# Cross-attention block with an MLP in f32: fc_w's forty-nine-product operands made during attention, and one fc scheme for all four MLP groups

## The chip, the cores and the metric

The kernel runs on one core of a Trainium2 chip. The metric is device time in microseconds; lower is better. All arithmetic is in f32. PE is the matrix engine (TensorE), PEld its weight loads, DVE the vector engine, ACT the scalar engine, POOL the GpSimd engine; SP issues the DMAs, and SPq is its queue.

## The reference

A transformer layer with cross-attention over 8 sequences of 256 tokens, width 512, 16 heads of 32, and an MLP of inner width 2048. Here x and ctx are [8, 256, 512]:

```python
y = layer_norm(x, ln1_w, ln1_b)
q = y @ q_w + q_b                      # [8,256,512] -> 16 heads of 32
k, v = ctx @ k_w + k_b, ctx @ v_w + v_b
attn = softmax(q @ k^T / sqrt(32) + mask)
hidden = (attn @ v) @ cproj_w + cproj_b + x
y = layer_norm(hidden, ln2_w, ln2_b)
y = gelu(y @ fc_w + fc_b, approximate=True)     # fc_w [512, 2048]
return hidden + y @ proj_w + proj_b             # proj_w [2048, 512]
```

## The kernel before

The 2048 tokens are worked in four groups of 512 (two sequences each). The kernel has two phases: attention for all four groups, and then the MLP for all four groups.

**Matrix products.** A product of two matrices cut into quarters is made with seven quarter products in place of eight (Winograd's form of Strassen's scheme). The left operand's quarters are 11, 12, 21, 22; `A_SUMS` makes from them four sums, called s3, s2, (a new) 21 and s4, and `B_SUMS` makes t1, t2, (a new) 12 and t4 of the right operand. `sum_up(eng, x, table, i)` issues sum i on the engine given. An operand of seven parts for 512 × 512 weights is a tile [128, 7, 2, 256], 1792 KB in all.

fc is a product of fc_w with the group's y. In group 0 of the MLP it is made column quarter by column quarter of fc_w (`fcw[0]` to `fcw[3]`): for each of four quarters q, seven products of 16 matmuls with 256 token columns. In groups 1 to 3 the scheme is applied twice: seven outer products of seven inner ones, 49 in all, each of 4 matmuls with 128 token columns. The profile shows two rows for every f32 matmul: 224 rows for the 7 × 4 × 4 of group 0, 392 for the 49 × 4 of another group. For these, fc_w's operands are the outer seven sums, each with its own inner seven parts: `w2`, seven operands of 1792 KB. They are made during group 0's MLP by `split_sums` on DVE and POOL through a stage tile `w_stage`, stored to `w2_dram` (L979, L980) and by `keep_quarters` (L989, L990), and loaded by `load_w2(g, k)` (L1004 to L1008) after each outer product for the product four further on.

**Buffers.** The weight pool has one tag with four buffers of 1792 KB. In attention they hold kw, qw, vw and cw (cproj_w); then come the four `fcw`, then `w2`.

**Attention.** It is a loop over 32 units n = (group g, head group hg, sequence b), eight units u = 2·hg + b for each group. A unit makes the scores of unit n+2 on PE (L575), softmaxes on DVE and ACT (L593, L603), a division on POOL (`divide`, L617), transposes of the probabilities on PE (`turn_probs`, L628), and the product with v (`attend`, L644; ACT writes it into the attention buffer, L652). The order is written out by hand: `aside[g, u, i]` holds work to be issued in slot i of a unit, and `between[g, u, i]` holds pieces of the projections for PE. `begin(g, u, i, f)` appends to a slot:

```python
for n, (g, hg, b) in enumerate(units):
    scores(n + 2); softmax(n + 2, 0)
    run(aside[g, u, 0])
    turn_probs(n, 0); turn_probs(n, 1); divide(n + 1)
    softmax(n + 2, 1); softmax(n + 2, 2)
    run(between[g, u, 0])
    turn_probs(n, 2); turn_probs(n, 3)
    run(aside[g, u, 1]); softmax(n + 2, 3)
    run(between[g, u, 1]); run(aside[g, u, 2])
    attend(n)
    run(later); run(aside[g, u, 3])
```

Each engine works through its instructions in this order. SP issues all DMAs, also in this order, and there are at most eight in flight: the issue of a DMA waits for the one eight before it. Keys, queries and values are stored to DRAM by `store_quarter` (L423) and loaded by `load_qk` (L511) and `load_v` (L516) for the head group that needs them. The attention output of group 1 is spilled (`spill_att`, L699) and reloaded chunk by chunk into `att_in` (`reload_att`, L704); its sums are made on POOL (L171), and `sum_att` (L664) makes those of a group whose output stays. The output projection (cw) of groups 1 and 2 runs as pieces in the fourth group's units. The residual x is loaded in quarters (`load_res`, L546), gets its bias on POOL (`bias_res`, L552) and is stored as `hid_dram` (L560). In the fourth group, hid of group 0 is loaded again (`hm`, L179), normalised on DVE and turned, to be y of MLP group 0.

**MLP.** For each group: fc (lines L926 on PE, L929 for the additions on DVE and POOL), gelu on ACT, then the product with proj_w, whose sums `pw_sums` are made during group 0. proj_w is loaded at the phase's start (L935). `add` and `mm` are helpers, so that many operations stand under one line and are told apart by their tiles.

Of the kernel before, what the change touches and what calls it, by code (L numbers as in the profile page):

```python
# [16 lines left out]
P = 128  # L17
# [5 lines left out]
def tile_xattn_block(  # L23
# [78 lines left out]
    }  # L102
    att_dram = tc.dram_tile([P, NHG, G], F32, name="att_dram")
# [37 lines left out]
    def weight(name, w, f=0):  # L141

        a = Operand(wts.tile([P, 7, HC, S], F32, tag="w", bufs=4, name=name))
        load_quarters(a, w, f, QUARTERS)
        return a

    def load_quarters(a, w, f, which):
        step = HI if w.shape[1] > D else S
        src = w.rearrange("(c p) n -> p c n", p=P)
        for n, k, at in (("11", 0, 0), ("12", HC, 0), ("21", 0, 1), ("22", HC, 1)):  # L150
            at = f + at * step
            if n in which:
                nc.sync.dma_start(a[n], src[:, k : k + HC, at : at + S])

# [81 lines left out]
    ys, hids, fcw = {}, {}, {}  # L236
# [15 lines left out]
    with ExitStack() as att:  # L252
# [98 lines left out]
        turns, later, waiting = [0], [], []  # L351
# [404 lines left out]
        for g in range(NG):  # L756
# [8 lines left out]
        spread(0, [(6, 2), (6, 2), (7, 2), (7, 2)], [lambda i=i: sum_up(GP, ws["c"], A_SUMS, i) for i in ALL])  # L765
# [14 lines left out]
            [(u, i, 1) for u in range(8) for i in range(2) if (u, i) not in ((6, 1), (7, 1))],  # L780
# [15 lines left out]
        for c, (u, i) in enumerate(((6, 1), (6, 1), (7, 1), (7, 1))):  # L796
            between[g, u, i].append(lambda c=c: th(c))

        def load_fc(q):
            fcw[q] = weight(f"fcw_{q}", fc_w, q * S)  # L800

        for q in (0, 2, 1):
            begin(g, 0, 3, load_fc, q)
        spread(
            g,
            [(2, 2), (2, 3), (4, 2), (5, 2)],
            [lambda i=i: sum_up(GP, fcw[0], A_SUMS, i) for i in ALL],
        )
# [7 lines left out]
        for t in range(12):  # L816
            nc.tensor.transpose(warm[:, ts(t % NT, P)], ident, ident)

        ws["k"] = Operand(wts.tile([P, 7, HC, S], F32, tag="w", bufs=4, name="kw"))
        ctxs[0] = load_tiles(  # L820
            work, group_of(ef, 0), "ctx", "ctx_0", lambda: load_quarters(ws["k"], k_w, 0, ("11", "12"))
        )
        load_quarters(ws["k"], k_w, 0, ("21", "22"))
        load_x(0)
        ws["q"] = weight("qw", q_w)
        load_mask(0)
        ws["v"] = weight("vw", v_w)
        for to, vec in ((cb, cproj_b), (projb, proj_b)):
            nc.sync.dma_start(to, vec.partition_broadcast(P))

# [5 lines left out]
        ws["c"] = weight("cw", cproj_w)  # L836
# [61 lines left out]
        sum_att(3, NHG - 1, V)  # L898
        for i in ALL:
            run(o[i : i + 1])  # L900
            sum_up(V, ys[0], B_SUMS, i)
# [3 lines left out]
        load_fc(3)  # L905


    with ExitStack() as mlp:
# [25 lines left out]
        for n, f, d in (("11", 0, 0), ("12", 0, HD2), ("22", HF, HD2), ("21", HF, 0)):  # L934
            nc.sync.dma_start(  # L935
                pw[n], proj_w.rearrange("(c p) n -> p c n", p=P)[:, f : f + HF, d : d + HD2]
            )

        def sum_pw():
# [12 lines left out]
        pw_sums = sum_pw()  # L952
        pbd = wpool.tile([P, HD2], F32, name="pbd")
        add(GP, pbd, projb[:, :HD2], projb[:, HD2:], ALU.subtract)

        w2_dram = tc.dram_tile([7, P, 7, HI // 2], F32, name="w2_dram")
        stage = wpool.tile([P, 3, 4, S], F32, tag="y2", bufs=1, name="w2_stage")
        FC_ORDER = (  # L960
            ("11", "11"), ("12", "21"), ("s2", "t2"), ("s3", "12"), ("21", "t1"), ("s4", "22"), ("22", "t4")
        )
        stages, staged_sums = [0], {}

        def split_sums(eng, n, r, half=None):
            a, b = fcw[r][n], fcw[r + NQF // 2][n]
            if half != 1:
                staged_sums[n, r] = stage[:, stages[0] % 3]
                stages[0] += 1
            st = staged_sums[n, r]  # L970
            s1, s2, s3, s4 = (st[:, i, :] for i in range(4))
            if half != 1:
                add(eng, s3, a[:, 0, :], b[:, 0, :], ALU.subtract)
                add(eng, s2, b[:, 1, :], s3, ALU.subtract)
            if half != 0:
                add(eng, s1, s2, a[:, 0, :])
                add(eng, s4, a[:, 1, :], s2, ALU.subtract)
                to = w2_dram[QI[n]][:, :, r * S : (r + 1) * S]
                nc.sync.dma_start(to[:, 2, :], s1)  # L979
                nc.sync.dma_start(to[:, 4:7, :], st[:, 1:, :])  # L980

        def keep_quarters(q):

            r = q % (NQF // 2)
            for c in range(HC):
                if q < NQF // 2 or c:
                    i = c if q < NQF // 2 else 3
                    to = w2_dram.rearrange("n p i s -> p n i s")[:, :, i, r * S : (r + 1) * S]
                    nc.sync.dma_start(to[:, 4:7], fcw[q].t[:, 4:7, c, :])  # L989
                    nc.sync.dma_start(to[:, 2], fcw[q].t[:, 2, c, :])  # L990

        w2 = {}

        def load_w2(g, k):
            t = wts.tile([P, 7, HC, S], F32, tag="w", bufs=4, name=f"w2_{g}_{k}")
            t = t.rearrange("p i h s -> p i (h s)")
            n = FC_ORDER[k][0]
            src = w2_dram[QI[n]]
# [452 lines left out]
```

## Time and profile before

| | before |
|---|---|
| time, median of 3 runs | 734.74 us (733.26 to 734.89) |
| the profiled execution's own time | 734.6 us |
| its span | 732.8 us |
| attention phase, from the start | 0 to 346.3 us |
| fc of MLP group 0 | 346.3 to 399.4 us |
| fc of MLP groups 1, 2, 3 | about 43.8 us each |
| projection of each MLP group | about 50 us |
| DMA over the span | 117.82 MB |

The span is the stretch from the first to the last instruction that the profile has; the profiled execution took 1.8 us more. PE busy counts matmuls, with weight loads (PEld) apart, since they run beside them. A row of the groups gives count, busy time and mean duration, and then the idle time of the engine just ahead of these instructions and what ended it. Rows of SPq are the issuing of DMAs; when a DMA landed is another column.

### The profile page before, as it was taken

What the parts mean: (1) busy time and instruction counts of PE and PEld (TensorE: products, weight loads), DVE (VectorE), ACT (ScalarE), POOL (GpSimd) and SP (SyncE); (2) the same over time, 40 slices, a digit from 0 to 9 for tenths busy, and PEclk for the clock granted to TensorE, in tenths of its full rate; (3) what the DMA queues carried; (4) which work ended last, traced back from release to release, by engine and by line L of the source; (5) the groups of instructions that cost most, each with busy time, mean ns of one, the idle gap of its engine ahead of it and who ended that gap; (6) DMA issues with size and microseconds to landing.
All of it is one profiled execution on the core that took longest, in us unless ns stands there. A gap on an engine that the chain in (4) does not pass through costs nothing.

```text
span 732.8 us, 13636 instructions
## 1 busy us (share of the span) xinstructions
PE 724.0 (99%) x4941; PEld 626.1 (85%) x4941; DVE 408.5 (56%) x1056; ACT 312.6 (43%) x888; POOL 480.3 (66%) x441
## 2 busy tenths in 40 slices
PE   9999999999999999999998999999999999999998
PEld 7888778888777787778877889998899988999886
DVE  4576756676456566866366595780156811666211
ACT  2277778766677788761332300225002160030500
POOL 3857689777564469996958970589404895048870
PEclk9999999999999999999999999999999999999999
DMA  9714422642234177533976982992019930172001
GB/s 300 250 59 134 159 90 93 208 148 87 87 102 164 59 204 245 186 115 101 305 256 217 305 324 77 388 319 93 1 58 354 350 115 1 58 270 89 1 1 57
DMA packets 79714, 117.82 MB, mean 161 GB/s; under 512 B 6644, under 2 KB 58400, under 8 KB 77984
## 3 DMA queue, kind: packets, MB, share of 16 engines
q1 hardware_dynamic: 79392, 116.94, 46.7%
q8 instruction: 39, 0.64, 0.4%
q14 instruction: 27, 0.22, 0.1%
q0 software_dynamic: 256, 0.02, 0.0%
HBM read 85.48 MB, written 31.46 MB: 160 GB/s over the span
## 4 chain that ended last, share of the span: by engine, by line
PE 93%; DMA 2%; DVE 2%; SPq 1%; POOL 1%; issue 1%; ACT 0%; DVEq 0%
PE py L926 26%; PE pf L926 19%; PE ppt L628 8%; PE pv L370 7%; PE po L370 7%; PE pqT L370 7%; PE pkT L370 5%; PE s L575 5%; PE av L644 4%; PE pkT L467 2%; DMA hm<-hid_dram 1%; PE pxt L217 1%; PE pyt L217 1%; SPq L935 1%; PE pct L217 1%; DMA kw<-in_L_xattn_k_w_dram 1%
## 5 line engine op out<-in xcount | busy, mean ns | idle before, releaser
L617 POOL TENSOR_TENSOR pr<-pr,rsum 128x512 f32<-128x512 f32 x128 | 130.2, 1049 | 68.6 <-DVE rsum L615 39.9
L929 POOL TENSOR_TENSOR h<-h,hs 128x512 f32<-128x512 f32 x79 | 98.9, 1275 | 104.2 <-DVE hs L929 103.6
L603 ACT ACTIVATE pr<-pr,nmax 128x256 f32<-128x256 f32 x256 | 127.7, 502 | 37.3 <-DVE nmax L593 37.1
L926 PEld LDWEIGHTS pf<-y,w 128*128 128x128 f32 x1176 | 131.8, 192 | 0.2
L926 PE MATMUL pf<-y,w 128*128 128x128 f32 x1176 | 131.8, 275 | 0.0
L593 DVE CUSTOM_DVE_ANT_0 pr<-s,mb 128x256 f32<-128x256 f32 x256 | 93.5, 413 | 39.7 <-PE s L575 31.3
L926 PE MATMUL py<-pw,h 128*128 128x256 f32 x384 | 84.9, 379 | 0.0
L926 PE MATMUL py<-pw_t,h 128*128 128x256 f32 x384 | 84.2, 379 | 0.0
L926 PEld LDWEIGHTS py<-pw_t,h 128*128 128x128 f32 x384 | 72.7, 190 | 9.8
L1264 ACT COPY u<-pf 128x512 f32<-128x512 f32 x21 | 12.3, 586 | 161.0 <-PE pf L926 161.0
L926 PEld LDWEIGHTS py<-pw,h 128*128 128x128 f32 x384 | 72.5, 190 | 9.6
L628 PEld LDWEIGHTS ppt<-ident,pr 128*128 128x128 f32 x512 | 57.5, 141 | 14.6 <-issue 9.3
L628 PE MATMUL ppt<-ident,pr 128*128 128x128 f32 x512 | 68.5, 276 | 0.2
L929 DVE TENSOR_TENSOR resm<-py,resm 128x512 f32<-128x512 f32 (+1 forms) x21 | 13.6, 663 | 83.9 <-PE py L926 83.9
L633 ACT COPY pt<-ppt 128x512 f32<-128x512 f32 x96 | 51.8, 574 | 7.1 <-PE ppt L628 7.1
L926 PE MATMUL pf<-y,fcw 128*128 128x256 f32 x224 | 49.8, 382 | 3.4 <-DVE u L929 2.2
L370 PE MATMUL pv<-vw,ctxT 128*128 128x256 f32 x224 | 52.4, 380 | 0.0
L929 DVE TENSOR_TENSOR u<-pf,u 128x512 f32<-128x512 f32 x50 | 34.5, 690 | 30.9 <-PE pf L926 25.6
L926 PEld LDWEIGHTS pf<-y,fcw 128*128 128x128 f32 x224 | 42.0, 190 | 11.1 <-DVE u L929 3.0
L370 PE MATMUL pqT<-xnT,qw 128*128 128x256 f32 x224 | 51.0, 379 | 0.0
L603 ACT ACTIVATION_READ_ACCUMULATOR pr<-pr,nmax 128x1 f32 x256 | 48.8, 191 | 0.0
L370 PEld LDWEIGHTS pqT<-xnT,qw 128*128 128x128 f32 x224 | 41.3, 190 | 5.1 <-issue 0.2
(142 smaller groups left out, 1138.4 us busy)
## 6 DMA issues: line engine op xcount, KB each, us to landing
w<-w_dram SPq DMA_DIRECT2D x12, 1792.0 KB, 8.0
w<-in_L_xattn_fc_w_dram SPq DMA_DIRECT2D x27, 256.0 KB, 5.6
w<-w_dram SPq DMA_DIRECT2D x9, 768.0 KB, 7.5
w_dram<-w_stage SPq DMA_DIRECT2D x14, 384.0 KB, 2.9
ctx<-in_ctx_dram SPq DMA_DIRECT2D x16, 256.0 KB, 4.5
x<-in_x_dram SPq DMA_DIRECT2D x16, 256.0 KB, 4.7
v_dram<-st_v SPq DMA_DIRECT2D x16, 256.0 KB, 2.2
v<-v_dram SPq DMA_DIRECT2D x16, 256.0 KB, 3.7
```

The lines of the kernel that those rows point to most:

```text
L217: nc.tensor.transpose(ps[:, ts(t, P)], xt[:, ts(c, P)], ident)
L370: nc.tensor.matmul(bank[n][:, i, :], l[:, c, ts(i, P)], r[:, c, :], start=first and i == 0 and c == 0, stop=last and c == HC - 1, skip_gro ...
L467: nc.tensor.matmul(bank[:, i, :], w[f"{n[0]}{j + 1}"][:, c, ts(i, P)], x()[f"{j + 1}{n[1]}"][:, c, :], start=at == 0, stop=j == 1 and c == ...
L575: nc.tensor.matmul(banks[j][:, i, :], qT[j * HD : (j + 1) * HD, b * S + i * P : b * S + (i + 1) * P], kT[j * HD : (j + 1) * HD, b * SK : ( ...
L593: nc.vector.tensor_tensor_reduce(pr[:, j, i, :], banks[j][:, i, :], mbias[g][1][:, b, :], scale=-SCALE, scalar=FLT_MAX, op0=ALU.add, op1=A ...
L603: nc.scalar.activation(pr[:, j, i, :], pr[:, j, i, :], AF.Exp, bias=nmax[:, j, i : i + 1], scale=-1.0, accum_out=sums[:, j, i : i + 1],)
L617: nc.gpsimd.tensor_tensor(pr[:, j], pr[:, j], rsum[:, j, :, None].to_broadcast([P, NQ, SK]), ALU.mult,)
L628: nc.tensor.transpose(ps[:, kc, ts(i, P)], probs[n][:, j, i, ts(kc, P)], ident)
L633: nc.scalar.copy(pt, ps)
L644: nc.tensor.matmul(av[j * HD : (j + 1) * HD, :], vs[g, hg][:, b * NK + kc, ts(j, HD)], pts[n, j][:, kc, :], start=(kc == 0), stop=(kc == N ...
L926: nc.tensor.matmul(ps, lhsT, rhs, start=first, stop=last, skip_group_check=True)
L929: eng.tensor_tensor(to, a, b, op)
```

## The change

The seven operands of fc_w for 49 products are made during attention, in buffers that are idle there, and group 0 of the MLP uses the same branch as groups 1 to 3. `fcw`, `split_sums`, `keep_quarters`, the stage tile and the branch with column quarters are gone.

- The weight pool has four named places in place of four buffers of one tag: k, q, v and c.
- Group 0 of attention: `fc["a"]` lies in place c, `fc["b"]` in the second attention buffer and the tile of its sums. Quarters 11 and 21 of fc_w are loaded, b = 11 − 21 is made on POOL, and 11 is split (four `A_SUMS` on DVE); its sums are stored (`keep_own`). 22 is loaded over a, a = 22 − b is the outer s2, stored as its first four parts (`keep_first_s2`); b is split and stored as s3 (`keep_s3`).
- Group 1: s2 is split and stored whole (`keep_all`, 1.835 MB). cproj_w is loaded into place c only now (unit 1, slot 3), and its four sums are made on POOL in units 2 and 3 rather than in group 0; they are kept in `cw_dram` (`keep_c`). 11 is then loaded into place c, and s2 comes back into the tiles of the residual.
- Group 2: the outer 21 and s4 are made from these in place c, split and stored whole. Quarter 12 is also loaded into place q (`fc["d"]`) and split on POOL, 22 into place k (`fc["e"]`) and split on DVE; their sums are stored. At unit 5, slot 3, ahead of `reload_att` and `load_res` in the same slot, `reload_c` loads cproj_w's quarters a second time and its sums from `cw_dram` into place c.
- Group 3: the first MLP operand is loaded into place k in unit 2; the second is `fc["d"]` as it lies in place q. The loads of three `fcw` and four POOL sums are gone. y of group 0 is turned one unit earlier, and its four `B_SUMS` move to DVE in units 6 and 7. Between the last four pieces of the output projection `split_y` runs on DVE (four sums of three quarters) where the `B_SUMS` were.
- MLP: after each outer product `load_w2` loads the next operand into the place that the product has left; places k, q and c take turns, and v joins after the first piece of group 0's projection. In its inner parts an operand that equals a quarter of fc_w is loaded from fc_w (three parts) and `w2_dram` (four). proj_w's quarters are loaded after the fourth and fifth products of group 0, and eight of the `pw_sums` follow the seventh.

The core of the diff:

```diff
-    a = Operand(wts.tile([P, 7, HC, S], F32, tag="w", bufs=4, name=name))
+    return Operand(wts.tile([P, 7, HC, S], F32, tag=f"w{at}", name=name))
...
-        spread(0, [(6, 2), (6, 2), (7, 2), (7, 2)], [lambda i=i: sum_up(GP, ws["c"], A_SUMS, i) for i in ALL])
...
+        def keep_c():
+            nc.sync.dma_start(cw_dram[:, 0], ws["c"].t[:, 2])
+            nc.sync.dma_start(cw_dram[:, 1:], ws["c"].t[:, 4:7])
+
+        def reload_c():
+            ws["c"] = place("cw_2", "c")
+            load_quarters(ws["c"], cproj_w, ("11", "12", "22"))
+            nc.sync.dma_start(ws["c"].t[:, 2], cw_dram[:, 0])
+            nc.sync.dma_start(ws["c"].t[:, 4:7], cw_dram[:, 1:])
+
+        begin(1, 1, 3, load_c)
+        spread(1, [(2, 3), (3, 1), (3, 2), (3, 2)], [lambda i=i: sum_up(GP, ws["c"], A_SUMS, i) for i in ALL])
+        begin(1, 4, 3, keep_c)
+        begin(2, 5, 3, reload_c)
...
+        def keep_all(key, n):
+            nc.sync.dma_start(w2_dram[QI[n]], rows_of(fc[key].t))
+
+        def keep_own(key, n):
+            keep_sums(n, rows_of(fc[key].t))
...
+        begin(0, 0, 3, fc_first)
+        sums([(0, 2, 1, GP), (0, 2, 1, GP), (0, 2, 2, GP), (0, 2, 2, GP)], "b", "a", "b", ALU.subtract)
+        split("a", V, (0, 2, 2), (0, 2, 3), (0, 3, 3), (0, 4, 0))
+        begin(0, 4, 1, keep_own, "a", "11")
+        begin(0, 5, 0, fc_load, "a", "22")
+        sums([(0, 5, 3, V), (0, 6, 1, GP), (0, 6, 1, GP), (0, 6, 2, V)], "a", "a", "b", ALU.subtract)
+        begin(0, 6, 3, keep_first_s2)
+        split("b", V, (0, 6, 3), (0, 7, 0), (0, 7, 2), (0, 7, 3))
+        begin(0, 7, 3, keep_s3)
+        split("a", V, (1, 0, 0), (1, 0, 2), (1, 0, 3), (1, 0, 3))
+        begin(1, 1, 0, keep_all, "a", "s2")
+
+        begin(1, 5, 3, fc_load, "c", "11")
+        begin(1, 6, 1, s2_again)
+        sums([(1, 7, 3, V), (1, 7, 3, V), (2, 0, 1, GP), (2, 0, 2, GP)], "c", "c", "s2", ALU.add)
+        split("c", V, (2, 1, 0), (2, 1, 2), (2, 1, 3), (2, 1, 3))
+        begin(2, 2, 0, keep_all, "c", "21")
+        begin(2, 2, 3, fc_load, "c", "12")
+        sums([(2, 3, 1, GP), (2, 3, 1, GP), (2, 3, 2, GP), (2, 3, 2, GP)], "c", "c", "s2", ALU.subtract)
+        begin(2, 3, 3, fc_load, "d", "12")
+        split("c", V, (2, 4, 0), (2, 4, 2), (2, 4, 3), (2, 4, 3))
+        begin(2, 5, 0, keep_all, "c", "s4")
+        split("d", GP, (2, 4, 2), (2, 4, 2), (2, 5, 1), (2, 5, 2))
+        begin(2, 6, 0, keep_own, "d", "12")
+        begin(2, 4, 3, fc_load, "e", "22")
+        split("e", V, (2, 6, 2), (2, 6, 3), (2, 7, 2), (2, 7, 3))
+        begin(3, 0, 0, keep_own, "e", "22")
+
+        def first_w2():
+            load_w2("k")
+            w2[w2_order.pop(0)] = rows_of(fc["d"].t)
+            w2_place[0, 1] = "q"
+
+        begin(NG - 1, 2, 0, first_w2)
...
-            [(u, i, 1) for u in range(8) for i in range(2) if (u, i) not in ((6, 1), (7, 1))],
+            [(u, i, 1) for u in range(8) for i in range(2) if (u, i) not in ((5, 1), (6, 1))],
...
-        for q in (0, 2, 1):
-            begin(g, 0, 3, load_fc, q)
-        spread(
-            g,
-            [(2, 2), (2, 3), (4, 2), (5, 2)],
-            [lambda i=i: sum_up(GP, fcw[0], A_SUMS, i) for i in ALL],
-        )
+        spread(g, [(6, 2), (7, 1), (7, 2), (7, 2)], [lambda i=i: sum_up(V, ys[0], B_SUMS, i) for i in ALL])
...
         for i in ALL:
             run(o[i : i + 1])
-            sum_up(V, ys[0], B_SUMS, i)
+            split_y(0, y2, i)
         bias_res(3)
         run(o[4:])
         run(later)
-        load_fc(3)
+        load_w2("c")
...
-                    if k + 4 < 7:
-                        load_w2(g, k + 4)
-                    elif g + 1 < NG:
-                        load_w2(g + 1, k - 3)
+                load_w2(w2_place[g, k])
...
+            product(3, ("12", "21"))
+            if g == 0:
+                load_pw("11", "12", "22")
+            product(4, ("22", "12"), ("21", "21"))
+            if g == 0:
+                load_pw("21")
```

## The prediction

> **What bounds the kernel now.** I read the page's busy row first, then the windows by stage, the groups of instructions by form, the chain of waits, and last the timelines of SP, POOL and PE at one place. On the page:
>
> ```profile
> span 732.8 us, 13636 instructions
> PE 724.0 (99%) x4941; PEld 626.1 (85%) x4941; DVE 408.5 (56%) x1056; ACT 312.6 (43%) x888; POOL 480.3 (66%) x441
> L926 PE MATMUL pf<-y,w 128*128 128x128 f32 x1176 | 131.8, 275 | 0.0
> w<-w_dram SPq DMA_DIRECT2D x12, 1792.0 KB, 8.0
> ```
>
> TensorE is busy for 724.0 of 732.8 us, so it is the bound: a change saves what it takes from PE's work and idle time, and loses whatever new idle it brings. In the windows the columns are stretch, length, then busy time (instructions) of PE, PEld, DVE, ACT, POOL, then clock, DMA share and GB/s. The four rows are units 0 to 6 of the third token group's attention, attention of the fourth, the fc product of MLP group 0, and that of group 1:
>
> ```profile
> 207.00:277.00 70.00, 70.00 (x576) 55.46 (x575) 43.57 (x177) 52.09 (x171) 37.74 (x39) 1.00 0.45 141
> 277.00:333.90 56.90, 56.70 (x497) 43.71 (x489) 41.80 (x142) 40.69 (x131) 56.25 (x56) 1.00 0.53 172
> 346.30:399.40 53.10, 49.68 (x225) 42.03 (x225) 29.56 (x46) 15.48 (x33) 41.10 (x40) 1.00 0.76 253
> 449.50:493.30 43.80, 43.80 (x393) 43.79 (x393) 31.51 (x50) 10.76 (x23) 25.05 (x22) 1.00 0.83 308
> ```
>
> Both fc stages give the same values: group 0 in 53.1 us of which PE idles 3.4, group 1 in 43.8 with none. The groups by form give the causes, the chain the length of one later stage:
>
> ```profile
> L926 PE MATMUL pf<-y,fcw 128*128 128x256 f32 x224 | 49.8, 382 | 3.4 <-DVE u L929 2.2 <-DVE h L929 1.2
> 449.49 43.77 PE pf L926 x392
> ```
>
> The idle 3.4 us follow DVE, which in that stage also makes split sums. In attention PE has no slack, DVE and POOL have some, and POOL is full in the fourth group (56.25 of 56.90). The DMA queue moves 141 and 172 GB/s there, far below the 350 to 388 of the fullest slices of the page.
>
> **What the Trainium skill says.** "DMA: Bandwidth & Descriptors", Specifications, puts HBM at about 358 GB/s for one core: the trace roughly agrees, since 256 KB loads behind one another land 0.72 to 0.76 us apart (345 to 364 GB/s) and the fullest slices of the page reach 350 to 388. The same page, "Anatomy of one DMA", has it that DMA engines do not wait on semaphores, the issuing sequencer does: an unready store therefore holds back every later SP issue, as the 7.79 us row for three kT stores in SP's timeline at 246.25 agrees. "PSUM — Partial Sum Buffer", Engine versus sequencer instructions, calls the VectorE, ScalarE and GpSimdE queues strict FIFO: below, POOL stands 1.63 us at a sum for att_in with a divide queued behind.
>
> **The change part by part.**
>
> *Group 0's fc in 49 sub-products.* 224 matmul rows at 382 ns go, 392 at the other groups' rate come: 53.1 − 43.8 = **−9.3 us**, 5.9 of it work and 3.4 idle time. This is on the path whole. 44 POOL operations (12 fcw sums, 32 of staging) and 24 DVE ones leave this MLP too, but PE waited on none beyond the 3.4.
>
> *Sums in attention.* 28 DVE sums of 0.69 us (19.3 us) and 16 POOL sums of 1.27 (20.3) come in groups 0 and 2; the four cproj sums move from group 0 to group 1; four fcw sums leave group 3. Units there are 7 to 10 us long. DVE has 43.57 of 70 us busy in group 2 and gets 11 more; POOL has 37.74 and gets 12.7. Cover: idle time between softmaxes. Unit (2,1) is tightest for DVE, by my count 9.9 of 10.0 us. With the wait of the ACT write into the attention buffer for the third-place operand's stores (landing about 134.2 to 135 against a need at 134.3), I take **+0.3**, bounds 0 and 1.5. A gain isn't excluded from cw's load leaving the start, where PE idles 6.3 us, but that idle ends with kw's and ctx's loads, which come first either way: 0.
>
> *split_y.* Between the last four pieces of attention four DVE sums of 1.09 replace four of 0.68: 1.6 us against pieces of about 3, zero if DVE is idle there (it is), up to 1.6 otherwise.
>
> *y of group 0 turned one unit earlier, its four sums moved to DVE in units 6 and 7 of the fourth group.* The transposes are the same number. hm, which the normalisation on DVE reads from 289.7 on, lands by the FIFO working below about 296 rather than 287; shifted by the seam, DVE needs it at 295.1 and stands 0.8 us with softmaxes behind it. DVE is busy 41.8 of 56.9 us in this stage and takes that up: 0, bounds 0 and 2.
>
> *More DMA in attention.* About 24.7 MB come: seven fc quarters 7.34, four "own" stores and a first s2 stored and read back, the whole-operand stores of 1.835, cw kept and reloaded, w2(0,0). At 365 GB/s that is 68 us of queue time over 346 us, mostly in gaps. One place is crowded: the seam from the third to the fourth group. SP, POOL and PE there, before:
>
> ```profile
> 264.05 1.18 SPq L511 DMA_DIRECT2D qT<-qT_dram  x1
> 265.33 1.92 SPq L704 DMA_DIRECT2D att_in<-att_dram  x4
> 280.62 0.36 SPq L516 DMA_DIRECT2D v<-v_dram  x1
> 265.75 4.04 POOL L617 TENSOR_TENSOR pr<-pr,rsum 128x512 f32<-128x512 f32 x4 [3.20 <-DVE rsum L615]
> 271.41 1.27 POOL L171 TENSOR_TENSOR att_in<-att_in 128x512 f32<-128x512 f32 x1 [1.63 <-DMA att_in<-att_dram]
> 275.96 4.03 POOL L617 TENSOR_TENSOR pr<-pr,rsum 128x512 f32<-128x512 f32 x4
> 278.77 1.09 PE L628 MATMUL ppt<-ident,pr 128*128 128x128 f32 x8
> 284.12 1.07 PE L644 MATMUL av<-pt,v 128*32 128x256 f32 x16
> ```
>
> The divide at 275.96 ends its first part about 277.0; PE takes it at 278.77, so slack is 1.8 us. After the change SP's order is: four e loads (1.05 MB) from 257.2, keep_all of s4 (1.835 MB) about 259.1, v store, kT, qT, then reload_c, which overwrites the very buffer that s4's store reads. In a FIFO queue at 365 GB/s, with 2.2 us latency for a read and 1.4 for a write as this trace has them, s4 lands at 268.8. SP stands from 264.5 until then, issues five cw DMAs (2.3 us; 1.835 MB ahead of att_in), and att_in's issue begins at 271.1 rather than 265.3. Its second chunk, which released POOL at 271.4, lands near 277.7. POOL waits, the divide behind it is 5.6 to 6.3 us late, its first part is there near 282.6 and PE idles 282.6 − 278.8 = 3.8, plus 0.5 at the next part: **+4.3**. Next late is v_3_0 (load issued at 280.62 before): it stands behind the 1.05 MB keep_own of d and four v stores and lands about 289.5, against a need of 284.1 + 4.3 = 288.4: **+1.1**. Seam: **+5.4**. Bounds: 0 if the queue drains s4 by 265 or POOL's sum comes after the divide; 9.8 at 330 GB/s by the same working.
>
> *Three buffers instead of four for MLP operands.* The load after a product is for three products on. Product k of 6.25 us gives up its buffer when it ends, and 1.835 MB plus latency need 7.3 us against 12.5. But group 0 also gets proj_w there: 4 × 1.835 + 2 × 1.05 = 9.44 MB from 348.9 to the need at 377.6, 25.9 us at 365 GB/s of 28.7 and with latency nearly full: slack 0.7. I take **+0.5**, bounds 0 and 5 (308 GB/s, what group 1's stage averaged).
>
> *Removed loads and stores.* 3.15 MB of fcw in group 3 and 5.5 MB of w2 stores in the MLP go. PE waited on no operand there: 0.
>
> Sum: 732.8 − 9.3 + 5.4 + 0.5 + 0.3 = **729.7** of span. The profiled execution took 734.6, 1.8 more than its span, which gives **731.5 us**; the median before is 734.74, 0.14 above that execution. So 731.5 is −0.44%. About 0.3% (2.2 us) is what a measurement of this kernel can tell from no change: below 732.5 counts as faster, above 736.9 as slower.
>
> **The rivals.**
>
> *A: the seam is hidden (0.30).* If SP doesn't stand (s4's store is out of the way by 265) or POOL's slack and the order of its sums take the delay, only the gain is left: 732.8 − 9.3 + 1.8 = 725.3, up to 728.5 with small stalls. For it: the queue's fullest slice reaches 388 GB/s, and the window has a 0.45 DMA share. Against: the buffer's hazard is real in the order of instructions, and e's load and s4's store are 2.9 MB in one go.
>
> *B: slower, by the DMA queue's rate (0.20).* One mechanism: if the queue drains at 330 GB/s or less when stores and loads mix, s4 lands about 271, att_in near 282, and v_3_0 after 294: seam 9.8. The MLP operand loads then miss by 1.5 to 5. Sum: 734.6 − 9.3 + 9.8 + 1.5 (to 5) + 0.3 = 736.9 to 740.4. It decides at about 330 GB/s. For it: group 1's fc stage, which only loads operands, averages 308, and whole-operand loads took 8.0 us in the median, not 7.1. Against: that stage isn't short of operands, so its average isn't a limit.
>
> *C: DVE or POOL in attention is the place that hurts (within the forecast's chance).* If unit (2,1) or the moved cproj sums in group 1 delay a softmax, each gives 1 to 2 us with the seam standing: 732.5 to 735.
>
> *That it doesn't do what it says (under 0.02).* PE should show 392 matmul rows of 128 columns in group 0's fc; the instruction order of the changed kernel shows them.
>
> **How the numbers follow.** Forecast with C 0.50 (728.5 to 736), A 0.30, B 0.20. Point: 731.5, the forecast's own. Range 726 to 738: its lower end leaves out about 0.1 of A, its upper about 0.1 of B. Faster by over 0.3%: all of A's 0.30 and 0.26 of the forecast's 0.50, for 732.5 lies only 1.0 above the point, 0.56. Within: the other 0.24. Slower: B's 0.20.
>
> **What would show it.** Right: in the chain a single pf step of about 43.8 us for group 0 with no DVE idle before it; on SP a row for w<-cproj_w about 268 to 269 with idle ahead of it; POOL's idle before the att_in sum grown from 1.63 to about 7; a gap of PE before ppt at about 279. If PE idles nowhere near 279, rival A holds and the seam's step is wrong. If it idles over 8 us there, or pf in group 0 has idle time released by a DMA of w, B's rate is right. If DVE's softmax releases PE in units (2,1) or (1,3), C. The forecast is wrong in kind if group 0's fc takes more than 46 us with operands there in time.

## The result: slower by 2.3%, and the profile after

| | before | changed |
|---|---|---|
| median | 734.68 us (733.26 to 734.89, 4 runs) | 751.47 us (750.12 to 753.14, 4 runs) |
| profiled execution, its span | 734.6, 732.8 us | 751.89, 750.1 us |
| attention, up to the first matmul of group 0's fc | 346.1 us | 372.4 us |
| fc of group 0 | 53.1 us | 43.8 us |
| projection of group 0 | 50.1 us | 50.7 us |

The ratio is 1.0234 (95% interval 1.0209 to 1.0259). The forecast was 731.5 us, in a range of 726 to 738. The page of the changed kernel, in the order of the lines shown of before:

```profile
span 750.1 us, 14053 instructions
...
PE 728.0 (97%) x5109; PEld 630.2 (84%) x5109; DVE 450.6 (60%) x1086; ACT 314.9 (42%) x892; POOL 490.0 (65%) x430
...
L1097 PE MATMUL pf<-y,w 128*128 128x128 f32 x1512 | 169.6, 275 | 0.0
...
w<-w_dram SPq DMA_DIRECT2D x16, 1792.0 KB, 9.0
```

PE's busy time rose by 4.0 us though 5.9 us of matmul work had gone, and its idle time rose by 13.3. Busy time can hide waits: a lone scores matmul has a row of 0.37 us, sixteen in a row take 1.15 us together. From the first `attend` to that of unit 23 the matmuls are the same as before, their rows cover 7.6 us more, and the idle time grew by 5.6. The windows (stretch, length, then busy time of PE, PEld, DVE, ACT and POOL, the clock, DMA share, GB/s) are group 0's fc, most of the third group's attention with the fourth's start, and the rest of the fourth's:

```profile
372.59:416.36 43.77, 43.77 (x393) 43.77 (x393) 31.52 (x50) 12.01 (x24) 27.86 (x25) 1.00 0.98 363
220.00:290.00 70.00, 69.22 (x541) 53.56 (x543) 51.83 (x187) 51.99 (x170) 43.38 (x40) 1.00 0.61 210
303.00:360.00 57.00, 56.67 (x465) 43.69 (x464) 43.20 (x140) 38.80 (x124) 52.76 (x53) 0.98 0.49 160
```

The fc stage is what was forecast: 43.77 us without a gap. All the loss lies ahead of it. Where it arises is read by subtracting, unit by unit, the start of `attend` on PE in one trace from that in another:

| attend of unit | 3 | 9 | 14 | 22, 23 | 24 | 31 | fc of group 0 starts |
|---|---|---|---|---|---|---|---|
| changed minus before, us | 0.9 | 8.4 | 10.0 | 12.8 | 25.3 | 26.0 | 26.3 |

So 12.8 us are lost before the seam, all but 1.6 of it in group 0, the first two units of group 1 and group 2, where additions were put (the 1.6 come at unit 14, with a long mask); 12.5 at the seam from the third to the fourth group; 1.0 in the fourth; then fc gives 9.3 back and the projection costs 0.6.

The seam in the timelines of SP, POOL and PE (start, duration, engine, line, operation, out<-in, count, and in brackets the idle time ahead and its releaser):

```profile
272.65 0.38 SPq L883 DMA_DIRECT2D w_dram<-w_c  x1
...
277.10 0.45 SPq L571 DMA_DIRECT2D qT<-qT_dram  x1
284.56 1.41 SPq L156 DMA_DIRECT2D cw<-in_L_xattn_cproj_w_dram  x3
...
287.00 2.93 SPq L764 DMA_DIRECT2D att_in<-att_dram  x4
```

```profile
278.55 4.04 POOL L677 TENSOR_TENSOR pr<-pr,rsum 128x512 f32<-128x512 f32 x4 [0.63 <-DVE rsum L675]
296.95 1.26 POOL L217 TENSOR_TENSOR att_in<-att_in 128x512 f32<-128x512 f32 x1 [14.37 <-DMA att_in<-att_dram]
...
301.43 4.03 POOL L677 TENSOR_TENSOR pr<-pr,rsum 128x512 f32<-128x512 f32 x4
```

```profile
302.53 2.11 PE L688 MATMUL ppt<-ident,pr 128*128 128x128 f32 x8 [10.86 <-POOL pr L677]
```

It is the forecast's mechanism, larger. SP has issued all it may by 277.55 and stands 7.0 us for the store of s4 (issued 272.65, landed 284.53), because the reload overwrites that buffer. att_in is issued at 287.0, its second chunk lands at 296.8, POOL stands 14.37 us with a divide behind, PE 10.86. And the eight ppt matmuls then take 2.11 us instead of 1.09: the clock granted to PE falls (0.77 in the mean of 290 to 300 us, 0.72 in the next 10; 0.50 in the window from 295.5 to 305.5). The seam's 12.5 us are 1.6 more than these 10.9, and 3 us of matmul rows at half the clock account for about that much. The chain of waits goes the same way:

```profile
272.65 11.88 DMA w_dram<-w_c
...
286.01 0.47 SPq L836
...
287.47 9.35 DMA att_in<-att_dram
...
296.95 1.26 POOL att_in L217
```

Ahead of the seam there is no such hole, but many small ones. In the timelines of DVE and then of POOL in the changed kernel, about units 5 and 6, stand these:

```profile
105.36 4.33 DVE L332 TENSOR_SCALAR mb<-mu 128x512 f32<-128x512 uint8 x1
...
119.93 0.69 DVE L563 TENSOR_TENSOR st_v<-pv,pv_u 128x512 f32<-128x512 f32 x1 [2.10 <-PE pv L430]
120.54 1.76 DVE L872 TENSOR_TENSOR w_a<-w_a,w_b 128x512 f32<-128x512 f32 x1
122.22 1.75 DVE L217 TENSOR_TENSOR w_b_sums<-w_b 128x512 f32<-128x512 f32 x1
```

```profile
105.38 4.02 POOL L677 TENSOR_TENSOR pr<-pr,rsum 128x512 f32<-128x512 f32 x4
...
119.25 2.50 POOL L872 TENSOR_TENSOR w_a<-w_a,w_b 128x512 f32<-128x512 f32 x2
121.71 1.72 POOL L217 TENSOR_TENSOR xnT<-xnT 128x512 f32<-128x512 f32 x1
```

An addition that takes 0.69 us when POOL rests, and also beside POOL when one operand is in PSUM (st_v at 119.93), took 1.75 with two SBUF operands beside POOL, and POOL's xnT sum 1.72 instead of 1.27. Of the 28 added on DVE, 13 took 1.05 to 1.76; together they lasted 28.2 us, priced at 19.3. And the mask operation `mb`, which the change does not touch, lasted 4.33 us instead of 0.62, until 0.3 us after the end of POOL's row of four divides. Behind it on DVE stand softmaxes, and PE waits for their row maxima. In the kernel before, the mask had already waited: at 104.49 it stood 0.33 us until a divide ended at 104.82, and ended 0.28 us later. The groups by form show the mask in the kernel before and in the changed one:

```profile
L272 DVE TENSOR_SCALAR mb<-mu 128x512 f32<-128x512 uint8 x4 | 2.3, 574 | 0.0
```

```profile
L332 DVE TENSOR_SCALAR mb<-mu 128x512 f32<-128x512 uint8 x4 | 9.5, 2375 | 0.0
```

The Trainium skill has this in "SBUF — State Buffer", Who interferes with whom: "A DVE instruction with two SBUF inputs contends with a GpSimd instruction that reads SBUF", and its tensor_scalar can do so in another mode, if its operands meet conditions that no run here tests; the loser blocks for the whole instruction. The trace agrees for the additions, 0.69 to 1.76 us, though not for every one: at 93.44 us one kept its 0.69 us beside POOL's `x`. For the mask it shows more than that sentence, a wait through four instructions. The prediction did not use it, nor a row that the trace of the kernel before already had, of additions of this form in the MLP, six of the eight with POOL busy beside them and 1.67 to 1.75 us long:

```profile
L929 DVE TENSOR_TENSOR pw_t<-pw,pw_t 128x512 f32<-128x512 f32 x8 | 11.3, 1471 | 0.0
```

### The profile page after: what moved, and what is told of

Same layout as the page of the kernel before. It is cut to its first block, busy times and chain, and to the rows that moved or that the text cites. A ratio compares the mean times of both kernels' runs of the same rounds, so it can differ in the third digit from the quotient of the medians.

```text
span 750.1 us, 14053 instructions
## 1 busy us (share of the span) xinstructions
PE 728.0 (97%) x5109; PEld 630.2 (84%) x5109; DVE 450.6 (60%) x1086; ACT 314.9 (42%) x892; POOL 490.0 (65%) x430
## 4 chain that ended last, share of the span: by engine, by line
PE 72%; DVE 4%; DMA 3%; issue 2%; ACT 2%; POOL 1%; SPq 1%; DVEq 0%; ACTq 0%; POOLq 0%
PE py L1097 25%; PE pf L1097 23%; PE po L430 5%; PE ppt L688 5%; PE pkT L430 3%; PE s L635 3%; PE pv L430 3%; PE av L704 2%; PE pqT L430 2%; DMA w_dram<-w_c 2%; DMA att_in<-att_dram 1%; ACT pr L663 1%; PE pyt L263 1%; ACT h L1213 1%; DVE pr L653 1%
## 5 line engine op out<-in xcount | busy, mean ns | idle before, releaser
L1100 POOL TENSOR_TENSOR h<-h,hs 128x512 f32<-128x512 f32 x100 | 126.7, 1291 | 120.9 <-DVE hs L1100 120.6
L1097 PEld LDWEIGHTS pf<-y,w 128*128 128x128 f32 x1512 | 169.5, 192 | 0.2
L1097 PE MATMUL pf<-y,w 128*128 128x128 f32 x1512 | 169.6, 275 | 0.0
L653 DVE CUSTOM_DVE_ANT_0 pr<-s,mb 128x256 f32<-128x256 f32 x256 | 93.4, 412 | 25.0 <-PE s L635 18.4
L1269 ACT COPY u<-pf 128x512 f32<-128x512 f32 x28 | 16.4, 585 | 200.0 <-PE pf L1097 200.0
L688 PE MATMUL ppt<-ident,pr 128*128 128x128 f32 x512 | 70.6, 279 | 14.7 <-POOL pr L677 10.9
L1100 DVE TENSOR_TENSOR resm<-py,resm 128x512 f32<-128x512 f32 (+1 forms) x21 | 13.6, 664 | 93.0 <-PE py L1097 93.0
L1100 DVE TENSOR_TENSOR hs<-pf,u 128x512 f32<-128x512 f32 x72 | 49.6, 689 | 13.2 <-PE pf L1097 11.9
L1213 ACT ACTIVATE h<-h,cols 128x256 f32<-128x256 f32 x128 | 51.9, 494 | 10.4 <-POOL h L1100 10.4
L1100 DVE TENSOR_TENSOR u<-pf,u 128x512 f32<-128x512 f32 x56 | 38.7, 691 | 28.8 <-PE pf L1097 25.0
```

The costliest lines, as they stand in the source:

```text
L653: nc.vector.tensor_tensor_reduce(pr[:, j, i, :], banks[j][:, i, :], mbias[g][1][:, b, :], scale=-SCALE, scalar=FLT_MAX, op0=ALU.add, op1=A ...
L688: nc.tensor.transpose(ps[:, kc, ts(i, P)], probs[n][:, j, i, ts(kc, P)], ident)
L1097: nc.tensor.matmul(ps, lhsT, rhs, start=first, stop=last, skip_group_check=True)
L1100: eng.tensor_tensor(to, a, b, op)
L1213: nc.scalar.activation(h[n][:, :, p, :], h[n][:, :, p, :], AF.Gelu_apprx_tanh, bias=col(c_fcb, half * HF + p), scale=1.0,)
L1269: nc.scalar.copy(u1, bank[1])
```

## The experiments

The table has the shift of `attend` against the kernel before, in us, in each kernel's profiled execution. Where that execution lies off the median, the shifts carry the argument and the medians only the total. Up to unit 18 the changed kernel, e1, e4 and e6 issue the same instructions, yet their shifts there are 11.9, 12.7, 13.3 and 14.7 us. In e1, e4 and e6 the clock granted to PE fell behind the first long mask (0.50 from 114.2 to 117.3 us in e1, 0.50 from 112.4 to 119.2 in e6); in the changed kernel's execution it stayed at 1.00 there. So a difference of up to 3 us between two shifts shows nothing by itself. In e3 and e5 the clock was 1.00 up to the seam. At unit 0 the shifts are −0.4 to 0.4 us, in e12 1.3.

| kernel | median | unit 9 | unit 14 | unit 23 | unit 24 | unit 28 | group 0's fc starts |
|---|---|---|---|---|---|---|---|
| changed | 751.47 | 8.4 | 10.0 | 12.8 | 25.3 | 25.3 | 26.3 |
| e1, reload later | 750.58 | 9.4 | 10.8 | 13.6 | 20.5 | 22.1 | 23.0 |
| e2, no additions | 740.48 | 0.2 | 4.9 | 4.9 | 16.2 | 16.2 | 17.1 |
| e3, mask on ACT | 747.28 | 6.0 | 6.0 | 8.9 | 18.5 | 18.5 | 19.5 |
| e4, places exchanged | 748.31 | 10.0 | 11.4 | 14.3 | 18.4 | 21.0 | 22.5 |
| e5, e3 with statistics | 742.33 | 3.1 | 3.2 | 4.4 | 16.9 | 16.9 | 17.9 |
| e6, seam cleared | 744.74 | 11.3 | 12.8 | 15.0 | 15.2 | 17.4 | 19.4 |
| e7, additions moved as well | 744.15 | 10.2 | 10.2 | 12.9 | 14.6 | 17.1 | 19.1 |
| e8, placed anew | 741.07 | 4.9 | 5.1 | 8.2 | 8.9 | 9.4 | 10.4 |
| e9, e8 without additions | 733.36 | 0.6 | 0.6 | 1.3 | 2.0 | 2.5 | 3.5 |
| e10, e8 mended | 737.33 | 4.7 | 4.8 | 8.3 | 8.7 | 8.7 | 9.7 |
| e11, e9 mended | 730.46 | 0.2 | 0.2 | 0.2 | 1.1 | 2.1 | 3.0 |
| e12, mask shifted in the kernel before | 734.96 | 1.8 | 1.8 | 1.8 | 1.8 | 1.8 | 1.8 |

**e1: the output weight's second load later.**

```diff
-        begin(2, 5, 3, reload_c)
...
         begin(g, 5, 3, load_res, 1, "11", "22", "21")
+        begin(g, 5, 3, reload_c)
```

> The changed kernel with the second load of the output weight issued behind the att_in and residual loads of the same slot, rather than ahead of them. Theory S (SP stands at the reload until the store of s4 has landed, and att_in waits behind it): att_in is issued about 277.6 instead of 287.0, its second chunk lands near 287 instead of 296.8, PE's idle time before ppt falls from 10.9 to 0 to 3 us and the clock does not drop; some 1 to 3 us come back where the pieces of the output projection wait for the weight: 739 to 743. Rival Q (the DMA queue is simply full there and order does not matter): att_in still lands after 293 and the time stays above 748.

Measured: 750.58 us (748.63 to 751.85), ratio 1.0216 (1.0197 to 1.0235). Theory S is right about att_in: it is issued at 278.9, its second chunk lands at 288.1, and PE's wait before ppt is 2.2 us instead of 10.9. It is wrong about the time, which hardly moved. Two of PE's waits in e1:

```profile
PE av L704 <- DMA v<-v_dram: 2.7, 1, 2.7
...
PE ppt L688 <- POOL pr L677: 2.2, 1, 2.2
```

The reload and the stores of d's sums now stand between att_in and v: v's load is issued at 301.7 where in the kernel before it was 280.6. The clock falls here too (0.83 from 290 to 310 us). Of the seam's 12.5 us 8.5 are left (13.6 to 22.1). What SP's order took from att_in, the bytes take from v.

**e2: the additions left out.**

```diff
-            nc.sync.dma_start(w2_dram[QI[n]], rows_of(fc[key].t))
+            nc.sync.dma_start(w2_dram[QI[n]][:, :4], rows_of(fc[key].t)[:, :4])
+            nc.sync.dma_start(w2_dram[QI[n]][:, 4:7], rows_of(fc[key].t)[:, 0:3])
...
-        sums([(0, 2, 1, GP), (0, 2, 1, GP), (0, 2, 2, GP), (0, 2, 2, GP)], "b", "a", "b", ALU.subtract)
-        split("a", V, (0, 2, 2), (0, 2, 3), (0, 3, 3), (0, 4, 0))
...
```

> The changed kernel without 40 of the 44 additions made for fc_w's operands in attention (those of fc d stay); the same bytes are loaded and stored (two stores of an operand are cut in two), so the operands hold unsummed quarters. Theory V (the sums on DVE and POOL, and their hold on each other, cost the 12.8 us that the units before the seam lose): the attend of unit 22 comes 8 to 12.8 us earlier, 739 to 744. Rival D (the added DMA traffic delays keys, queries and values there): 748 or more.

Measured: 740.48 us, ratio 1.0081 (1.0053 to 1.0109). Up to unit 13 the kernel stands within 0.2 us of before, with all the added DMA: rival D falls. The 4.9 at unit 14 come with the second mask, which here lasted 5.58 us (from 181.77; in the kernel before 0.62 from 181.53), and the clock fell behind it (0.50 from 191.7 to 194.9). So the long mask needs no additions. The seam still costs 11.3.

**e3: the mask on ACT.**

```diff
-            nc.vector.tensor_scalar(mb, mu, -1.0, FLT_MAX, ALU.add, ALU.mult)
+            if g == 0:
+                nc.vector.tensor_scalar(mb, mu, -1.0, FLT_MAX, ALU.add, ALU.mult)
+            else:
+                nc.scalar.activation(mb, mu, AF.Identity, bias=neg_max, scale=FLT_MAX)
```

> The changed kernel with the mask of groups 1 to 3 made on ACT (one activation) instead of DVE. Theory M (two of the mask operations took 4.33 and 4.14 us instead of 0.62 because POOL ran beside them, and these lost 2.9 and 1.3 us of PE time): 747 to 748.5. Rival (the stretched operation stands in time that DVE would have idled anyway): 750.5 to 752.

Measured: 747.28 us, ratio 1.0182 (1.0160 to 1.0203). The mask takes 0.73 us on ACT each time, the shift before the seam falls from 12.8 to 8.9. Theory M holds with 3.9 us, about what was expected (4.2). That price is for an execution without a fall of the clock behind the mask; in e1, e4 and e6 unit 6, with the first long mask, cost 1.7 to 2.8 us more than in the changed kernel.

**e4: the places exchanged.**

```diff
-            ws["c"] = place("cw_2", "c")
+            ws["c"] = place("cw_2", "k")
...
-        begin(2, 5, 3, reload_c)
+        begin(2, 4, 3, reload_c)
...
-        begin(2, 5, 0, keep_all, "c", "s4")
+        begin(2, 6, 0, keep_all, "c", "s4")
...
-        begin(2, 4, 3, fc_load, "e", "22")
...
+        begin(3, 0, 3, fc_load, "e", "22")
...
```

> The changed kernel with the places exchanged: the output weight comes back into place k at unit (2,4), where no store is waited for; the store of s4 goes behind the att_in and residual loads (unit 2,6); fc e is loaded into place c in group 3, unit 0, and split there in units 2 to 4. Theory S: no SP wait at the reload; att_in about as early as in the kernel before plus the 12.8 us of shift; PE does not idle before ppt: 738 to 741. Rival Q: still over 5 us idle there, 744 or more. The sums of e in group 3 may cost 0 to 2 us.

Measured: 748.31 us, ratio 1.0201 (1.0167 to 1.0234). PE no longer waits before ppt, so SP's wait is what held att_in. But 2.9 MB of stores (s4, d) now stand ahead of v, and PE waits there:

```profile
302.50 1.93 PE L704 MATMUL av<-pt,v 128*32 128x256 f32 x16 [4.02 <-DMA v<-v_dram]
```

Both theories have a share. Here, too, the clock fell: 0.83 in the window from 300 to 310 us, in which this idle stretch ends.

**e5: statistics in place of additions.**

```diff
+        def fake(*places):
+            for g, u, at in places:
+                begin(g, u, at, lambda: nc.vector.bn_stats(dummy, ws["v"].t[:, 0].rearrange("p h s -> p (h s)")))
...
-        split("a", V, (0, 2, 2), (0, 2, 3), (0, 3, 3), (0, 4, 0))
+        fake((0, 2, 2), (0, 2, 3), (0, 3, 3), (0, 4, 0))
...
```

> The changed kernel with the mask on ACT, and each of the 28 additions on DVE in attention replaced in its slot by a statistics instruction over one 128x512 operand (0.68 us, one SBUF input instead of two); the 12 POOL additions stay, the bytes moved are the same, the operands hold unsummed quarters. With real additions in these slots (mask on ACT) the time was 747.3 us and the attend of unit 22 came 8.9 us late. Theory L (what costs is that an addition with two SBUF inputs and POOL exclude each other, so that both are stretched): unit 22 comes 0 to 2.5 us late, 738 to 741. Theory F (the time in DVE's queue itself): as late as with additions, 745 to 748.

Measured: 742.33 us, ratio 1.0108 (1.0086 to 1.0129). The groups by form have the substitutes at 0.69 us throughout:

```profile
L908 DVE BATCH_NORM_STATS2 dummy<-vw 128x6 f32<-128x512 f32 x28 | 19.3, 689 | 0.4
```

At the same slots of unit 6, DVE's timelines of e3 and of e5 read:

```profile
118.12 1.76 DVE L877 TENSOR_TENSOR w_a<-w_a,w_b 128x512 f32<-128x512 f32 x1
119.81 1.75 DVE L219 TENSOR_TENSOR w_b_sums<-w_b 128x512 f32<-128x512 f32 x1
```

```profile
118.55 1.41 DVE L908 BATCH_NORM_STATS2 dummy<-vw 128x6 f32<-128x512 f32 x2
```

The shift before the seam is 4.4 us, neither L's 0 to 2.5 nor F's 8.9: about half of the additions' 8.9 us goes when the DVE instructions read one SBUF operand and keep their length beside POOL; the other half stays with 28 DVE instructions of 0.69 us and the 12 POOL additions in their queues (e2 up to unit 13 and e9, with the same DMAs and shifts of 0.2 and 0.6 us, show that the DMAs have no part in it). The substitutes also wait for no load and no POOL result. In e3 only one of the 28 additions waited over 0.2 us for such a thing: 3.0 us, until 109.32, for the load of 22. From unit 5 to unit 6, across that wait, the shift grew by 0.6 us in e3 and in e5 alike, so it is not the difference. The substitutes write 6 columns rather than 512; whether reads or writes hold each other up is not separated.

**e6: the seam cleared.**

```diff
+            ws["c"] = place("cw_2", "q")
...
+        begin(2, 3, 3, reload_c)
...
+        begin(3, 2, 0, fc_load, "d", "12")
...
+        begin(3, 0, 1, keep_all, "c", "s4")
+        split("d", V, (3, 3, 0), (3, 3, 3), (3, 4, 0), (3, 4, 3))
...
```

> The changed kernel with the seam cleared: the output weight comes back into place q at unit (2,3); the store of s4 goes behind the loads of v and hm at the start of group 3; quarter 12 is loaded into place c and split on DVE in group 3 (units 3 and 4) rather than in group 2. The exchange of places before this (e4) still waited 4.0 us for v behind the stores of s4 and d. Theory S+Q (the wait of SP and the 2.9 to 4 MB that are queued ahead of att_in and v make the 12.5 us together): the shift of units 23 to 24 falls from 12.5 to 0 to 2 us, 738 to 742. Rival: a new wait of more than 4 us at the seam, 744 or more.

Measured: 744.74 us, ratio 1.0141 (1.0118 to 1.0163). The seam costs 0.2 us (15.0 to 15.2) instead of 12.5, and SP's timeline has v's load at 295.2 ahead of the stores:

```profile
279.51 1.97 SPq L764 DMA_DIRECT2D att_in<-att_dram  x4
...
295.19 0.36 SPq L576 DMA_DIRECT2D v<-v_dram  x1
...
298.51 0.43 SPq L883 DMA_DIRECT2D w_dram<-w_c  x1
```

So the 12.5 us are SP's wait and the queued bytes together. The total is above what was expected, for two reasons: d's additions in the fourth group, where POOL has no rest, came with a loss of 3.9 us from unit 24 to unit 31 (0.7 in the changed kernel), and the shift before the seam was 15.0 in this execution, with the clock at 0.50 for 6.8 us behind the first mask.

**e7: the additions moved as well.** With e6's seam and e3's mask:

```diff
+        sums([(0, 6, 0, V), (0, 6, 0, V), (0, 6, 3, V), (0, 7, 0, V)], "a", "a", "b", ALU.subtract)
...
+        split("b", V, (0, 4, 0), (0, 4, 3), (0, 5, 0), (0, 5, 3))
```

> e6_seam with the mask on ACT and the additions of groups 0 and 2 moved to slots in which POOL has little queued (before the reciprocal and after the attend of a unit), those of s2 all on DVE. Theory L: the shift before the seam falls from 12.8 to 2 to 6 us, 729 to 735. Theory F (moving them does not help, DVE's time is what counts): 8 us or more of shift, 736 or more.

In this kernel b is split before a = 22 − b is formed, and the split replaces a quarter of b, so its s2 is another matrix; the number of operations is the same. Measured: 744.15 us, ratio 1.0130 (1.0113 to 1.0148). A miss: the first split, moved to unit 2, made PE wait 4.5 us for DVE, and 12.9 us were lost before the seam. By the number this is theory F's, but the split's second addition on DVE (87.32 us) had itself stood 2.5 us for a POOL addition of b, so this run does not tell L from F.

**e8: placed anew.** From the changed kernel:

```diff
+                nc.scalar.activation(mb, mu, AF.Identity, bias=neg_max, scale=FLT_MAX)
...
+            ws["c"] = place("cw_2", "k")
...
+        begin(2, 4, 3, reload_c)
...
+        split("a", V, (0, 3, 0), (0, 3, 3), (0, 4, 0), (0, 4, 3))
...
+        sums([(0, 6, 0, V), (0, 6, 0, V), (0, 6, 3, V), (0, 6, 3, V)], "a", "a", "b", ALU.subtract)
...
+        split("b", V, (0, 7, 0), (0, 7, 0), (0, 7, 3), (0, 7, 3))
...
+        begin(3, 0, 1, keep_all, "c", "s4")
...
+        begin(3, 1, 0, keep_own, "d", "12")
...
+                if (g, k) == (0, 5):
+                    sum_up(V, last_own[0], A_SUMS, 0, 1, 2, 3)
```

> A version made from what the runs showed. Mask on ACT; the output weight comes back into place k at unit (2,4) with nothing to wait for; the stores of s4 and of d's sums go behind v and hm in group 3; the additions of groups 0 and 2 lie ahead of a unit's reciprocal or behind its attend, those of d at the end of group 2; quarter 22 (e) is loaded and split only in the MLP, in product 6 of group 0. Accounts: the shift before the seam 8.9 us with the mask on ACT, of which half is the exclusion between DVE and POOL and should mostly go (3 to 5 left), seam 0 to 1, group 3 0.7, group 0's fc 43.8 plus 0 to 1.5: 729 to 733. If the exclusion moves along with the additions, 735 to 738.

Measured: 741.07 us, ratio 1.0091 (1.0078 to 1.0105). Seam and mask are gone as expected, the additions are not: 7.7 us at unit 22, and 13 of 30 on DVE still took over 1 us. The exclusion moves along with them. e's four additions took 4.86 us in a row, and group 0's fc 46.6 instead of 43.8.

**e9: e8 without the additions in attention,** left out as in e2; d's four stay.

> e8_placed without the additions for fc_w's operands in attention except d's four (operands hold unsummed quarters; the bytes moved are the same). If the three costs (additions, mask, seam) are the whole loss, what is left is the gain of group 0's fc and small waits: 725 to 728. If DMA traffic or the order of loads costs more that these hid, 730 or more.

Measured: 733.36 us, ratio 0.9986 (0.9979 to 0.9992). Attention is only 3.5 us longer than before. That the time is not 728 lies in group 0's fc: 48.2 us. PE waited 2.3 us there for DVE, which had e's additions in front, and its clock was 0.83 from 390 to 400 us.

**e10 and e11: e's additions spread over product 6;** e10 is e8 with that and some additions moved once more, e11 is e9 with that alone.

```diff
                 made("22", 5, u3)
+                e_sum(k, 0)
...
+                e_sum(k, 1)
                 sub(7, "22", "t4", False, True)
                 made("21", 7, u2)
+                e_sum(k, 2)
                 sub(5, "s4", "22", False, True)
                 made("12", 5, u2)
+                e_sum(k, 3)
```

> e8_placed with e's four additions spread over product 6 of group 0, one behind every second sub-product (in e8 the four stood in a row for 4.85 us and PE idled 2.3 us); the additions of a = 22 - b half a unit earlier, those of s4 on DVE instead of POOL, d's four no longer in group 3. Group 0's fc 43.8 to 44.5 instead of 46.6; shift before the seam 4 to 6.5 us instead of 7.7: 732 to 737. If exclusion moves along again, 737 to 740.

> e9_floor (without the additions in attention but d's) with e's additions spread as in e10. Group 0's fc 43.8 to 44.5 instead of 48.2: 728 to 729.5. If that stage still takes over 46, its three buffers or the loads of proj_w are a cost of their own.

Measured: e10 737.33 us, ratio 1.0034 (1.0022 to 1.0047), at the upper end of what was expected; e11 730.46, ratio 0.9937 (0.9923 to 0.9950), 1 us above its range. Group 0's fc takes 45.2 us in both. e11 closes the account: with neither additions in attention (but d's four), nor the long mask, nor the seam, 4.2 us of the 9.3 are left over after 3.0 lost in attention, 1.4 in group 0's fc, where e's additions stand, and 0.7 in the projection. Where the 3.0 come from was not taken apart. e10 minus e11, 6.9 us, is what the other additions in attention cost, even placed as well as was tried. No version with them beats the kernel before.

**e12: the mask shifted in the kernel before.**

```diff
+            if g:
+                nc.vector.bn_stats(dummy, cb[:, :S])
             nc.vector.tensor_scalar(mb, mu, -1.0, FLT_MAX, ALU.add, ALU.mult)
```

> The kernel before with one small statistics instruction (128x256, about 0.35 us) on DVE right ahead of the mask of groups 1 to 3, nothing else changed. Theory M (whether the mask gets its turn against POOL's row of divides depends on a few tenths of a microsecond of timing, and the changed kernel only shifted it): at least one of the three masks takes 3.5 to 5.6 us instead of 0.62, each such one costs 1 to 4.5 us: 736 to 743. Rival (the long masks came from the added additions or DMAs): all stay below 1 us and the time at 734 to 735.5.

Measured: 734.96 us, ratio 1.0009 (1.0000 to 1.0017). A miss for theory M, and not the rival's case either: the masks took 1.28, 1.29 and 0.41 us. Each waited for one divide at most, not for the row. That the long mask is POOL's doing rests on its ends: all nine long ones, in five kernels, end 0.28 to 0.29 us after a POOL row, as the short ones in the kernel before end 0.28 us after a divide. e3 shows what the long ones cost. What decides whether the mask waits for one operation or for all of them stays open.

## Why the prediction was wrong

- **Group 0's fc, −9.3 us:** right. 43.77 us, no gap, the same row length as the other groups. (The 224 rows of the kernel before are 112 matmuls, so 4 in each of the 28 products, not 16.)
- **Sums in attention, +0.3 us with bounds of 0 and 1.5:** this step failed most. It cost 12.8: 8.9 for the additions, 3.9 for the mask. The working priced an addition at 0.69 us and called DVE's idle time of a whole stage the cover (43.57 of 70 us busy). But beside POOL 13 of the 28 additions lasted 1.05 to 1.76 us, and a few tenths of a microsecond ahead of a reciprocal delay a divide or PE, whatever the stage's mean: PE waited 3.3 us, in four places, for DVE's `rsum` before the seam. The trace of the kernel before had the other price, 1.47 us in the mean of its `pw_t` row; an estimate from it for 28 additions is 41 us of DVE time instead of 19.3 (they took 28.2). The mask, which the change does not touch, was in no term. The bound of 1.5 looked only at the tightest unit by sums of durations. Rival C named this kind of loss, with 1 to 2 us each, but at other units: at (2,1) the shift grew by 0.5 us, at (1,3) by none, against 6.3 by the end of group 0.
- **Seam, +5.4 us with a bound of 9.8:** the mechanism was right from s4's store to PE, the size was off, 12.5. With the 12.8 of shift taken off, s4 landed 2.9 us later than worked out (e's loads ahead of it landed at 279.2), although it moved at 344 GB/s (1.835 MB in the 5.3 us from 279.2 to 284.5), near the 365 assumed. The five cw loads and att_in's first two took 12.3 us from SP's release (284.56 to 296.82) instead of 8.9: the queue moved 276 GB/s in that time, and only 190 in its start, from 284.5 to 287.3; why it was slower than 365 stays open. So att_in was 6.3 us later than worked out, and PE idled 10.9 us instead of 3.8. The clock's fall, 1.6, was in no term. v, put at +1.1, cost nothing here, hidden behind the longer wait, but came forward in e1 (2.7 us) and e4 (4.0 us).
- **Three buffers, +0.5 us:** the size is luck. The projection was 0.6 longer, but no operand was late in the fc stage, although the queue ran at 363 GB/s there, and PE's one wait over 0.2 us in the projection was 0.3 us for a sum on POOL (`hs`).
- **split_y and y's sums, 0 us:** 1.0 was lost from unit 28 on; three of the four y sums in units 6 and 7 took 1.59 to 1.75 us beside POOL, against a price of 0.68. That these cost the 1.0 is not shown.
- **Rival B** had the sign and a part of the seam: s4's store moved at 344 GB/s, above its line of 330, but the loads behind it at 276, below it. Its late operands in fc did not come, and it too had nothing for the additions, the largest loss.

Together: 12.8 + 12.5 + 1.0 − 9.3 + 0.6 = 17.6, against 17.3 between the spans.

## What to carry to other kernels

Idle time on DVE beside a busy POOL is not free for additions on two SBUF operands: take their price from rows of the trace in which such additions stand beside POOL (here 1.47 us in the mean, not 0.69), and look at what stands behind them in the queue, not at the stage's mean. A reload into a buffer that was still being stored made SP stand for 7.0 us, and everything later in its program with it; moving the reload alone (e1) handed the wait to the next load, so count the bytes ahead of each needed load as well. And when precomputation is moved into a stage where PE has no slack, first run that stage with the work left out and once more with it: here the difference, 6.9 to 8.9 us, ate most of the 9.3 gained.

## What was not expected of the hardware

- A mask of 0.62 us lasted 3.99 to 5.58 us in five kernels when it met a row of POOL operations, and stayed at 0.53 to 0.61 in another place of the same runs. Even the 0.62 was half a wait for a divide. e12 did not bring the long one about.
- The clock granted to PE fell to 0.50 for some 3 to 10 us at a time, and eight transposes then took 2.11 us instead of 1.09. It did not need a long idle stretch, and did not follow from a short one each time. In e9 it fell behind an idle stretch of 2.3 us (0.50 from 392.4 to 395.6 us), in e8 behind one as long it did not (1.00 from 395 to 405). Behind the first long mask PE's rows covered 3.55 of 5.00 us in e1 (107 to 112 us), with no idle stretch over 0.8, and the clock fell; in the changed kernel they covered 3.56 and it did not. The Trainium skill describes such a gate in "TensorE: Matmul & The Clock Gate", Part 1, with half the clock as its idle state, as these windows have it. In the kernel before, with no idle stretch over 1.35 us, its windows show 1.00.
